# Begin and change of phases of a two-layer graph network laid out anew

## The chip, the cores and the metric

The kernel runs on one core of a Trainium2 chip, in float32. The metric is the device time of one execution in microseconds. Five engines work side by side, each with its own queue of instructions in a fixed order: PE (TensorE: matrix products and transposes), DVE (VectorE), ACT (ScalarE), POOL (GpSimd), and SP (SyncE), which here only issues DMAs.

## The reference

The input `x` is 128 graphs of 64 nodes with 768 features; `adj` is a boolean 64 x 64 matrix for each graph. Both layers are wrapped in a residual and a layer norm.

```python
# layer 0: graph attention with 12 heads of 64, and a gate
h = einsum('bnd,ade->bane', x, W);  th = tanh(h)
a = einsum('bane,aeo->bano', th, w_src) + swap(einsum('bane,aeo->bano', th, w_dst))
a = softmax(where(adj, leaky_relu(a, 0.2), -999.0))
f = elu(einsum('banm,bame->bane', a, h) + b)
g = sigmoid(x @ H_w.T + H_b)
x = layernorm(x + g * f + (1 - g) * x)
# layer 1: self attention with 6 heads of 128
q, k, v = x @ Wq + bq, x @ Wk + bk, x @ Wv + bv
p = softmax(q @ k.T / sqrt(128) + where(adj, 0, -9e15))
x = layernorm(x + (p @ v) @ Wf + bf)
```

## The kernel before

**Tiling.** Two graphs make a tile of 128 tokens (64 tiles), two tiles a pair (32 pairs, numbered 0 to 31). The large products are not computed block by block but in schemes with fewer multiplications: x times [W | H_w] of a pair with 15 products of sums of blocks (class `Stream`, its matrix instructions at L428), x1 times W_v with 7 (class `Product`, L373). For these, sums of blocks are needed: sums over the activations ("S sums", `block_sum` L668 for [W | H_w], `token_sums` L456 for W_v) and sums over the weights (`weight15_sum` L331, 14 for each matrix; `weight_sums` L337, 12 for W_v). The activations' sums run on POOL.

**Two phases.** Phase A does, pair by pair, layer 0 and the product with W_v, whose result goes to DRAM. Phase B does the rest of layer 1, in groups of two pairs. In phase A a pair takes 22 "steps" of PE.

**The order** on every engine is written by hand. `at(step, f)` notes that f is to emit its instructions at a step; all events are sorted by step and run. The steps come from tables: `A_LEAD` and `A_TAIL` for the two tiles of a pair (attention: tanh, dst and src sums, mask, exponentials, scale, aggregate, gate, mix, norm), `A_PAIR` for what a pair shares (loads of x "xb_in", transposes "xT", S sums, loads and transposes of x1), and `MOVED`, offsets for single entries in pairs 0 to 3 and the last three. `BEGIN` holds the steps of the start, `SEAM` those of the change of phases. An engine executes strictly in the resulting order; a waiting instruction holds up all behind it.

**The begin.** Pairs 0 and 1 use plain products, since the weight sums aren't there yet: `plain` (L686) takes h of pair 0 from raw W, `plain_blocks` (L700) h of pair 1 from the blocks, `plain_g` (L715; evicted by DVE at L724) the gate of both. PE transposes H_w's six row blocks (`hw_blocks`, L602), which `load_hrow` (L586) stages in the tile `w2_all`. That tile also holds five blocks of H_w's transpose that the sums would overwrite (`kept_at`), for pair 1's gate, and later the 7 x 1152 columns for W_v and its sums (`weight_plain` L341 loads four blocks: slots 0, 1, 4 and 6). So W_v can load only when all that is no longer needed. Pair 2 is the first whose [W | H_w] product runs in the 15-product scheme, from weight sums made by DVE.

**Around a 15-product step.** Four PSUM tiles ("X") take turns. Each product is evicted by DVE (L746, L748, L757) or by ACT and DVE (L751, then L757), into the tiles xb (h) and hgp (gate). DVE also does the mask (L853), the row maximum (L857), reciprocals (L870), tile transposes of x (L634), the sums over tanh (L799, L808) and the normalization's statistics (L495 to L506). ACT adds (L846) and exponentiates (L862). POOL multiplies with w_dst and w_src (L796, L804), scales the probabilities (L872), and finishes rstd (L507 to L512). PE transposes the probabilities (L883) and aggregates (L901). Attention needs h of the other graph's half in the right partitions, by an exchange DMA (L832, L833), and dst transposed through DRAM (L814, L822).

**The change of phases.** The last pair uses the scheme for W and H_w apart. While its attention and the last two V products run, Wq and Wk load, and their sums (L331, 128 x 256) and those of the first x1 group (L480) are made, all by DVE. ACT then copies at L1437 and the q products (L428, evicted by ACT at L1200 and DVE at L1205) begin.

Of the kernel before, what the change touches and what calls it, by code (L numbers as in the profile page):

```python
# [16 lines left out]
P = 128  # L17
# [33 lines left out]
    -3: 2, 0: 0.5, -1: -1.0, -2: -3,  # L51
}
SEAM = {
    "wq": (15.2, 19.05, 21.41, 19.73, 15.24, 15.81), "wk": (23.61, 26.84, 27.25, 27.56, 31.16, 29.25),
    "wq_sums": (43.53, 43.53, 43.53, 43.53, 44.94, 45.97, 46.03, 46.1, 46.64, 46.71, 48.03, 48.48, 51.7, 53.88),
    "x_sums": (46.57, 48.69, 49.6, 55.88),
    "wk_sums": (51.23, 51.23, 51.93, 52.46, 53.21, 53.21, 54.94, 54.94, 55.54), "x1T": 41.88,
}
BEGIN = {
    "x1_turn": 2.3, "hw": (6.84, 8.48, 10.12, 12.38, 13.26, 14.39),  # L60
    "spread": (1.46, -1.26, -4.37, -2.42, -6.85, -5.31), "h0": (1.02, 3.49, 5.33, 6.0),
    "h1": (8.78, 10.35, 11.68, 13.08, 14.59, 15.89), "g0": (16.99, 17.87, 19.06, 19.8, 19.94, 21.07),
    "g1": (24, 26.46, 26.7, 28, 30.14, 30.91),
    "sums": (16, 16.4, 16.8, 17.2, 17.6, 18, 18.96, 19.36, 19.76, 20.16, 20.63, 21.03, 21.19, 22.66),
    "wv": (31, 30.99, 34.31, 32.04), "v_sums": (34.44, 37, 38, 40.19, 39.85, 40.46, 41.6, 42.47, 44, 45, 46, 47),
}
MOVED = {
    (0, "lead", "add0", None): -1.15, (0, "lead", "dst_in", None): 1.44, (0, "lead", "dst_out", None): 1.44,
    (0, "lead", "dst_sum", None): 1.44, (0, "lead", "exp1", None): 0.42, (0, "lead", "gate", None): 9,
    (0, "lead", "gate_in", None): 1.54, (0, "lead", "mix1", None): -0.33, (0, "lead", "norm1", None): 0.1,  # L70
    (0, "lead", "probs", None): -0.84, (0, "lead", "scale1", None): -0.34, (0, "lead", "src_mul", None): 0.91,
    (0, "lead", "src_sum", None): 1.44, (0, "pair", "S", 0): -2.05, (0, "pair", "S", 1): -2.05,
    (0, "pair", "S", 2): -0.53, (0, "pair", "S", 3): -2.05, (0, "pair", "S", 4): -2.05,
    (0, "pair", "S", 5): -0.11, (0, "pair", "S", 6): -2.05, (0, "pair", "S", 7): -3.68,
    (0, "pair", "S", 8): -2.05, (0, "pair", "S", 9): -2.05, (0, "pair", "S", 10): -2.05,
    (0, "pair", "adj", None): -1.45, (0, "pair", "load", None): 4.57, (0, "pair", "x1T0", None): 2.87,
    (0, "pair", "x1T1", None): 6.05, (0, "pair", "x1_in0", None): 2.1, (0, "pair", "x1_in1", None): 6.5,
    (0, "pair", "x1_sums", 0): 2.1, (0, "pair", "x1_sums", 1): 2.1, (0, "pair", "x1_sums", 2): 2.1,
    (0, "pair", "x1_sums", 3): 1.94, (0, "pair", "xT1", None): 2.9, (0, "pair", "xb_in1", None): 0.77,
    (0, "tail", "aggregate", None): -0.2, (0, "tail", "elu", None): -0.2, (0, "tail", "exchange", None): 0.58,  # L80
    (0, "tail", "gate", None): 8.98, (0, "tail", "norm1", None): 0.17, (0, "tail", "probs", None): -0.41,
    (0, "tail", "scale1", None): -0.2, (0, "tail", "src_sum", None): 2.73, (1, "lead", "add1", None): -0.14,
    (1, "lead", "aggregate", None): 1.47, (1, "lead", "cap", None): -0.86, (1, "lead", "dst_sum", None): 0.36,
    (1, "lead", "elu", None): 1.47, (1, "lead", "exchange", None): 0.15, (1, "lead", "exp0", None): -0.04,
    (1, "lead", "exp1", None): 0.36, (1, "lead", "gate", None): 1.09, (1, "lead", "mask", None): 0.07,
    (1, "lead", "mix1", None): 0.8, (1, "lead", "mix2", None): 0.81, (1, "lead", "probs", None): 1.11,
    (1, "lead", "scale0", None): 0.59, (1, "lead", "scale1", None): 0.59, (1, "lead", "src_mul", None): 0.09,
    (1, "lead", "top", None): 0.07, (1, "pair", "S", 0): -1.23, (1, "pair", "S", 1): 0.55,
    (1, "pair", "S", 2): -0.29, (1, "pair", "S", 3): -2.06, (1, "pair", "S", 4): -0.17,
    (1, "pair", "S", 5): -0.17, (1, "pair", "S", 6): -0.17, (1, "pair", "S", 7): -1.81,  # L90
    (1, "pair", "S", 8): -0.17, (1, "pair", "S", 9): -0.17, (1, "pair", "S", 10): -0.17,
    (1, "pair", "adj", None): -0.68, (1, "pair", "load", None): -1.86, (1, "pair", "x1T0", None): 0.97,
    (1, "pair", "x1_sums", 0): 1.03, (1, "pair", "x1_sums", 1): 1.03, (1, "pair", "x1_sums", 2): 1.03,
    (1, "pair", "x1_sums", 3): 2.18, (1, "pair", "xT0", None): -2.34, (1, "pair", "xT1", None): -0.02,
    (1, "pair", "xb_in0", None): -1.35, (1, "pair", "xb_in1", None): -1.22, (1, "tail", "add0", None): 2.16,
    (1, "tail", "aggregate", None): 0.24, (1, "tail", "cap", None): 2.61, (1, "tail", "dst_in", None): 0.5,
    (1, "tail", "dst_out", None): 0.52, (1, "tail", "dst_sum", None): 0.1, (1, "tail", "elu", None): 0.54,
    (1, "tail", "gate", None): 0.1, (1, "tail", "gate_in", None): 0.1, (1, "tail", "mix1", None): 0.24,
    (1, "tail", "mix2", None): 0.24, (1, "tail", "scale1", None): 1.95, (1, "tail", "spill", None): 0.81,
    (1, "tail", "src_mul", None): 0.1, (2, "lead", "add1", None): -0.55, (2, "lead", "dst_in", None): 0.63,  # L100
    (2, "lead", "dst_out", None): 0.63, (2, "lead", "dst_sum", None): -0.08,
    (2, "lead", "exchange", None): -1.38, (2, "lead", "exp1", None): 1.88, (2, "lead", "gate", None): 2.23,
    (2, "lead", "gate_in", None): 0.63, (2, "lead", "mix1", None): 0.3, (2, "lead", "mix2", None): 0.3,
    (2, "lead", "scale0", None): 0.97, (2, "lead", "spill", None): -0.1, (2, "lead", "src_sum", None): 0.63,
    (2, "lead", "top", None): -0.01, (2, "pair", "S", 0): 0.19, (2, "pair", "S", 1): 0.19,
    (2, "pair", "S", 2): -1.55, (2, "pair", "S", 3): 0.19, (2, "pair", "S", 4): 0.19, (2, "pair", "S", 5): 0.19,
    (2, "pair", "S", 6): 0.19, (2, "pair", "S", 7): 0.19, (2, "pair", "S", 8): 0.19, (2, "pair", "S", 9): 0.37,
    (2, "pair", "S", 10): -0.88, (2, "pair", "adj", None): -6.12, (2, "pair", "load", None): -5.68,
    (2, "pair", "x1T0", None): 0.21, (2, "pair", "x1T1", None): 0.21, (2, "pair", "x1_in0", None): 0.71,
    (2, "pair", "x1_in1", None): 0.47, (2, "pair", "x1_sums", 0): -0.33, (2, "pair", "x1_sums", 1): 0.77,  # L110
    (2, "pair", "x1_sums", 2): 0.33, (2, "pair", "x1_sums", 3): 0.77, (2, "pair", "xT0", None): -0.24,
    (2, "pair", "xb_in0", None): -0.85, (2, "pair", "xb_in1", None): 2.38, (2, "tail", "add0", None): -0.02,
    (2, "tail", "cap", None): 0.97, (2, "tail", "exchange", None): -0.38, (2, "tail", "gate_in", None): -1.09,
    (2, "tail", "mix2", None): 0.18, (2, "tail", "scale0", None): -0.07, (2, "tail", "src_sum", None): 1.37,
    (3, "lead", "add0", None): -2.45, (3, "lead", "gate_in", None): -2.42, (3, "lead", "mix2", None): -0.28,
    (3, "lead", "src_mul", None): 0.39, (3, "pair", "S", 0): -0.05, (3, "pair", "S", 2): -0.21,
    (3, "pair", "load", None): 1.23, (3, "pair", "x1_in0", None): 0.72, (3, "pair", "x1_sums", 0): 1.66,
    (3, "pair", "x1_sums", 1): 1.66, (3, "pair", "x1_sums", 2): 2.33, (3, "pair", "x1_sums", 3): 1.66,
    (3, "pair", "xT0", None): -1.11, (3, "pair", "xb_in0", None): 3.9, (3, "pair", "xb_in1", None): 3.34,
    (3, "tail", "aggregate", None): -0.19, (3, "tail", "cap", None): -2.28, (3, "tail", "dst_in", None): 0.41,  # L120
    (3, "tail", "dst_mul", None): -0.19, (3, "tail", "gate", None): 2.27, (3, "tail", "mix1", None): 0.04,
    (3, "tail", "src_mul", None): -0.33, (3, "tail", "src_sum", None): 1.34, (3, "tail", "tanh", None): -1.24,
    (4, "lead", "dst_mul", None): 0.11, (4, "lead", "exchange", None): -0.73, (4, "lead", "exp0", None): 0.05,
    (4, "lead", "exp1", None): 0.05, (4, "lead", "gate", None): 0.05, (4, "lead", "mask", None): 0.05,
    (4, "lead", "src_sum", None): 0.21, (4, "lead", "top", None): 0.05, (4, "pair", "S", 0): -0.26,
    (4, "pair", "S", 1): -0.26, (4, "pair", "S", 2): -0.26, (4, "pair", "S", 3): -0.26,
# [1424 lines left out]
```

## Time and profile before

| | us |
|---|---|
| time, median of 3 runs | 2821.89 (2819.24 to 2822.54) |
| the profiled execution | 2821.93 |
| its span | 2820.1 |
| PE busy in the span | 2775.9 |
| DVE busy | 1905.0 |
| POOL busy | 1495.9 |
| ACT busy | 1163.1 |

PE is busy for 98% of the span, and the chain that ended last lies on PE for 93%. The mean granted clock of PE was 0.995. A timeline row gives the start and the length of a run of like instructions, the engine, the line, output <- input with shapes, the count, and in brackets the idle time ahead with what ended it. Line numbers in this document are those of the kernel before.

### The profile page before, as it was taken

The numbers are of one execution on the slowest core, as the hardware profiler recorded it, in microseconds if no ns is written. First come the engines' busy times: TensorE is split into PE (matmuls) and PEld (weight loads), VectorE is DVE, ScalarE is ACT, GpSimd is POOL, SyncE is SP. The second block draws the span as 40 slices with busy tenths as digits, with TensorE's granted clock in tenths as the row PEclk, the third lists the DMA queues.
The fourth block names the chain that finished last, engine by engine and source line by source line (L and its number), as shares of the span: only waits on it lengthen the run. The fifth ranks groups of instructions, "written<-read, shape, count | busy, mean of one in ns | idle before, by whom it ended". The sixth has DMA issues, their size and how long they took to land.

```text
span 2820.1 us, 50020 instructions
## 1 busy us (share of the span) xinstructions
PE 2775.9 (98%) x17544; PEld 1958.7 (69%) x17544; DVE 1905.0 (68%) x4026; ACT 1163.1 (41%) x3685; POOL 1495.9 (53%) x1791
## 2 busy tenths in 40 slices
PE   8899999999999999999799999999999999999998
PEld 7445545555555555555578888888888888888887
DVE  4888888888888888888754555555555555555556
ACT  4466565665666665665622221122221222211223
POOL 1656556555555565565455645445645445554455
PEclk9999999999999999999899999999999999999999
DMA  5454454454454454444631221221221222211222
GB/s 147 126 151 136 136 152 130 133 154 131 133 157 134 133 150 132 140 150 132 174 130 35 91 81 65 70 91 58 91 73 63 80 65 84 91 68 58 91 85 74
DMA packets 358682, 308.36 MB, mean 109 GB/s; under 512 B 226592, under 2 KB 304160, under 8 KB 358432
## 3 DMA queue, kind: packets, MB, share of 16 engines
q1 hardware_dynamic: 358144, 304.77, 35.2%
q8 instruction: 140, 2.29, 0.3%
q14 instruction: 110, 0.90, 0.1%
q10 hardware_dynamic: 288, 0.39, 0.0%
HBM read 191.41 MB, written 101.06 MB: 104 GB/s over the span
## 4 chain that ended last, share of the span: by engine, by line
PE 93%; DVE 3%; DMA 1%; POOL 1%; ACT 1%; SPq 0%; issue 0%; POOLq 0%; DVEq 0%; ACTq 0%
PE X L428 70%; PE X L373 15%; PE pa L901 2%; PE pb L1326 2%; PE pb L1244 2%; PE pa L883 1%; PE pb L1302 1%; PE X L715 1%; PE X L700 1%; POOL Sc L1190 0%; DMA w<-in_L_gnn_Wv_dram 0%; DVE s L853 0%; ACT s L862 0%; DMA hb_bc<-in_L_gnn_H_b_dram 0%; DVE T L634 0%
## 5 line engine op out<-in xcount | busy, mean ns | idle before, releaser
L428 PE MATMUL X<-S,w 128*128 128x256 f32 x2752 | 636.5, 380 | 0.0
L428 PE MATMUL X<-w,S 128*128 128x512 f32 (+1 forms) x1364 | 598.9, 584 | 10.7 <-POOL S L668 7.5
L428 PEld LDWEIGHTS X<-S,w 128*128 128x128 f32 x2752 | 519.1, 190 | 68.5
L428 PEld LDWEIGHTS X<-w,S 128*128 128x128 f32 x1364 | 254.9, 191 | 289.8 <-issue 241.0
L1222 DVE TENSOR_TENSOR xs<-xs,X 128x256 f32<-128x256 f32 x512 | 209.6, 418 | 175.1 <-PE X L428 166.9
L872 POOL TENSOR_TENSOR s<-s,rs 128x384 f32<-128x384 f32 x128 | 106.9, 836 | 372.1 <-DVE rs L870 355.9
L428 PE MATMUL X<-w,Sc 128*128 128x256 f32 x1280 | 294.4, 381 | 0.1
L1205 DVE TENSOR_TENSOR k<-k,X 128x256 f32<-128x256 f32 x320 | 132.6, 417 | 232.4 <-PE X L428 160.6
L373 PE MATMUL X<-w,S 128*128 128x384 f32 x768 | 270.9, 490 | 1.5 <-POOL S L456 1.4
L428 PEld LDWEIGHTS X<-w,Sc 128*128 128x128 f32 x1280 | 241.5, 190 | 34.1 <-DVE xs L1222 0.9
L1205 DVE TENSOR_TENSOR q<-q,X 128x256 f32<-128x256 f32 x320 | 132.9, 419 | 195.0 <-PE X L428 155.0
L428 PE MATMUL X<-xb,w 128*128 128x256 f32 x1024 | 258.6, 383 | 0.8 <-ACT q L1200 0.8
L862 ACT ACTIVATE s<-s,nmx 128x64 f32<-128x64 f32 x768 | 254.8, 335 | 6.8 <-DVE nmx L857 6.8
L516 ACT ACTIVATE xs<-xs,shift,rstd 128x768 f32<-128x768 f32 x62 | 63.5, 1025 | 435.8 <-POOL shift L512 416.0
L428 PE MATMUL X<-w,T 128*128 128x512 f32 (+1 forms) x496 | 223.9, 583 | 5.7 <-DVE xb L757 3.4
L1200 ACT ACTIVATE k<-X,bk_c 128x256 f32<-128x256 f32 x192 | 90.9, 473 | 316.4 <-PE X L428 316.4
L846 ACT ACTIVATE s<-s,src 128x64 f32<-128x64 f32 x768 | 196.6, 338 | 37.6 <-DMA s<-dst_d 34.2
L428 PEld LDWEIGHTS X<-xb,w 128*128 128x128 f32 x1024 | 192.2, 190 | 28.4 <-ACT q L1200 1.2
L757 DVE TENSOR_TENSOR hgp<-hgp,X 128x512 f32<-128x512 f32 (+1 forms) x235 | 150.6, 651 | 80.8 <-PE X L428 67.2
L1200 ACT ACTIVATE q<-X,bq_c 128x256 f32<-128x256 f32 x192 | 90.8, 473 | 276.7 <-PE X L428 276.7
L373 PEld LDWEIGHTS X<-w,S 128*128 128x128 f32 x768 | 141.1, 190 | 90.1 <-POOL S L456 1.6
L1190 POOL TENSOR_TENSOR w<-cT 128x256 f32<-128x256 f32 x32 | 23.3, 727 | 334.2 <-PE X L428 332.9
(143 smaller groups left out, 4893.1 us busy)
## 6 DMA issues: line engine op xcount, KB each, us to landing
xb<-in_x_dram SPq DMA_DIRECT2D x64, 384.0 KB
s<-dst_d SPq DMA_DIRECT2D x128, 192.0 KB
x_d<-xb SPq DMA_DIRECT2D x64, 384.0 KB
xT_d<-T SPq DMA_DIRECT2D x64, 384.0 KB
v_d<-v SPq DMA_DIRECT2D x128, 192.0 KB
xb<-xT_d SPq DMA_DIRECT2D x32, 768.0 KB
xb<-v_d SPq DMA_DIRECT2D x256, 96.0 KB
xs<-x_d SPq DMA_DIRECT2D x64, 384.0 KB
```

Source lines behind the costliest of these rows:

```text
L373: nc.tensor.matmul(o, self.lhsT(i, c), rhs, start=first and c == 0, stop=last and c == CH - 1, skip_group_check=True,)
L428: nc.tensor.matmul(ps, self.lhsT(r, slot, c), self.rhs(r, slot, c), start=start and c == 0, stop=stop and c == 1, skip_group_check=True,)
L516: nc.scalar.activation(r, r, AF.Identity, bias=shift, scale=rstd)
L757: nc.vector.tensor_tensor(o, o, view(ps), ALU.add if positive else ALU.subtract)
L846: nc.scalar.activation(self.s[:, a], self.s[:, a], AF.Prelu, bias=self.src[:, a : a + 1], alpha=LEAKY_ALPHA,)
L862: nc.scalar.activation(self.s[:, a], self.s[:, a], AF.Exp, bias=self.nmx[:, a : a + 1], accum_out=self.sm[:, a : a + 1],)
L872: nc.gpsimd.tensor_tensor(t, t, rs[:, :, None].to_broadcast([P, A // 2, S]), ALU.mult)
L901: nc.tensor.matmul(self.pos[h2][own, j, :], self.pt[rws, j, own], rhs, start=True, stop=True,)
L1200: nc.scalar.activation(o[:, b], ps, AF.Identity, bias=bias[:, hd : hd + 1], scale=1.0 if positive else -1.0)
L1205: nc.vector.tensor_tensor(o[:, b], o[:, b], ps, ALU.add if positive else ALU.subtract)
L1222: nc.vector.tensor_tensor(o, o, ps, ALU.add if positive else ALU.subtract)
L1244: nc.tensor.matmul(pc[own, q, i, j, :], qT[:, b, q, own], kT[:, b, q, own], start=True, stop=True,)
```

## The change

Four things change together.

1. `load_hrow` puts the rows 0 to 4 of H_w at offsets inside the slots that W_v's blocks take, and row 5 in a tile of its own; `kept_at` moves into slots that only W_v's sums take. W_v's loads then have to wait only for the transposes of rows 0 to 4, and their steps go from 31-34 to 16-19.
2. The four buffers "snap" become one tile "snaps" of the same size, whose quarters `snap` takes in turn. Pair 2's transposes of x go into it instead of into T tiles, and its loads of x, transposes and S sums come some ten steps sooner. A list of the loaded x tiles becomes an entry by tile; pair 1's second tile is loaded first.
3. Each weight sum has an engine: in the begin, 2 of the 14 sums of [W | H_w] go to POOL, and of W_v's 12, which were all on POOL, 4 go to DVE. In the change of phases 6 of the 14 sums for Wq, 5 of the 9 early ones for Wk and 1 of the 4 sums of x1 go from DVE to POOL.
4. The steps of BEGIN, SEAM and MOVED are new. On PE, the first transposes of H_w rows come ahead of the last h products of pair 0; the first two aggregations (L883, L901) move by some groups of the gate's products. For the last pairs, the mask L853 of a tile stands before two evictions instead of after, L799 and L801 before the statistics, rstd behind two L456, and the last exchange comes sooner. In the pairs between, the order is practically the old one.

```diff
-    -3: 2, 0: 0.5, -1: -1.0, -2: -3,
+    -3: 2, 0: 0.5, -1: 0.5, -2: -3,
...
 SEAM
-    "x_sums": (46.57, 48.69, 49.6, 55.88),
+    "x_sums": (47.3, 49.42, 52.14, 57.17),
...
+    "q_on": (0, 0, 1, 1, 1, 0, 0, 0, 1, 0, 1, 1, 0, 0), "x_on": (0, 1, 0, 0),
+    "k_on": (1, 1, 0, 1, 1, 0, 1, 0, 0),
...
 BEGIN
-    "x1_turn": 2.3, "hw": (6.84, 8.48, 10.12, 12.38, 13.26, 14.39),
+    "x1_turn": 1.91, "hw": (2.1, 5.84, 9.65, 13.05, 14.38, 15.55),
...
-    "wv": (31, 30.99, 34.31, 32.04), "v_sums": (34.44, 37, 38, 40.19, 39.85, 40.46, 41.6, 42.47, 44, 45, 46, 47),
+    "wv": (16.38, 18.07, 18.64, 16.34), "on": (0, 0, 0, 1, 0, 0, 0, 0, 1, 0, 0, 0, 0, 0),
+    "v_on": (1, 0, 1, 1, 0, 1, 1, 1, 0, 1, 1, 0),
+    "v_sums": (33, 33.8, 34.6, 35.4, 36.2, 37, 37.8, 38.6, 39.4, 40.2, 41, 41.8),
...
 MOVED
-    (2, "pair", "S", 2): -1.55, (2, "pair", "S", 3): 0.19, (2, "pair", "S", 4): 0.19, (2, "pair", "S", 5): 0.19,
+    (2, "pair", "S", 2): -11.5, (2, "pair", "S", 3): -9.76, (2, "pair", "S", 4): -9.76, (2, "pair", "S", 5): -9.76,
...
-    (2, "pair", "xT0", None): -0.24
+    (2, "pair", "xT0", None): -9.24, (2, "pair", "xT1", None): -9, (2, "pair", "xb_in0", None): -8.3,
...
         def load_hrow(oc):
-            hrows[oc] = w2_all[:, oc * D : (oc + 1) * D]
+            o = (0, D, 2 * D, 6 * D, 9 * D)
+            hrows[oc] = k3.tile([P, D], F32, name="pt") if oc == 5 else w2_all[:, o[oc] : o[oc] + D]
...
         def kept_at(slot):
-            t = w2_all[:, NC * D :]
             k = KEPT.index(slot)
-            return t[:, k * 512 : (k + 1) * 512].rearrange("p (c o) -> p c o", c=2)
+            o = 3 * D + k * 512 + (k == 4) * (7 * D + 384 - 3 * D - 4 * 512)
+            return w2_all[:, o : o + 512].rearrange("p (c o) -> p c o", c=2)
...
-        def turn(xp):
-
-            dst = k3.tile([P, NC, P], F32, name="T", bufs=4)
+        def turn(xp, dst=None):
+
+            if dst is None:
+                dst = k3.tile([P, NC, P], F32, name="T", bufs=4)
...
+        snaps = k1.tile([P, 4 * HALF], F32, name="snaps")
+        n_snap = [0]
+
         def snap(k, ps):
-            t = k1.tile([P, HALF], F32, name="snap", bufs=4)
+            n = n_snap[0] % 4
+            n_snap[0] += 1
+            t = snaps[:, n * HALF : (n + 1) * HALF]
...
-            at(BEGIN["sums"][n], lambda k=k: weight15_sum(whg, k, nc.vector, slice(0, 512)))
+            eng = (nc.vector, nc.gpsimd)[BEGIN["on"][n]]
+            at(BEGIN["sums"][n], lambda k=k, eng=eng: weight15_sum(whg, k, eng, slice(0, 512)))
...
-                    lambda c=c, k=k: weight_sums(lambda s: w2[:, s, c], nc.gpsimd, [k]),
+                    lambda c=c, k=k: weight_sums(
+                        lambda s: w2[:, s, c], (nc.vector, nc.gpsimd)[BEGIN["v_on"][4 * c + k]], [k]
+                    ),
...
             def xb_in(d, i):
-                d.setdefault("xp", []).append(blocks(x_t[2 * d["p"] + i]))
+                d["xb", i] = blocks(x_t[2 * d["p"] + i])
...
             def xT(d, i):
-                d.setdefault("T", []).append(turn(d["xp"][i]))
+                dst = snaps[:, i * D : (i + 1) * D].rearrange("p (c n) -> p c n", n=P) if d["p"] == 2 else None
+                d.setdefault("T", []).append(turn(d["xb", i], dst))
...
+        ENG = (nc.vector, nc.gpsimd)
...
-            at(o + SEAM["wq_sums"][k], lambda k=k: weight15_sum(early[0], k, nc.vector, slice(0, P)))
+            at(o + SEAM["wq_sums"][k], lambda k=k: weight15_sum(early[0], k, ENG[SEAM["q_on"][k]], slice(0, P)))
...
-            at(o + SEAM["x_sums"][k], lambda k=k: group_sum(early_sums, k, nc.vector, EARLY[k]))
+            at(o + SEAM["x_sums"][k], lambda k=k: group_sum(early_sums, k, ENG[SEAM["x_on"][k]], EARLY[k]))
...
-            at(o + SEAM["wk_sums"][k], lambda k=k: weight15_sum(early[1], k, nc.vector, slice(0, P)))
+            at(o + SEAM["wk_sums"][k], lambda k=k: weight15_sum(early[1], k, ENG[SEAM["k_on"][k]], slice(0, P)))
```

## The prediction

> **What bounds the kernel now.** I read the windows of busy time first, then the waits of PE, then the timeline of each engine around every wait of PE over 0.3 us. The profiled execution took 2821.93 us: a span of 2820.1 and 1.83 outside it. It stands 0.04 above the median of 2821.89, so a sum made against it holds for the median. PE is busy 2775.9 us of the span, which leaves 44.2 idle. The windows (columns: stretch, length, busy us of PE, PEld, DVE, ACT, POOL with instructions, clock, DMA share, GB/s) say where:
>
> ```profile
> 80.00:120.00 40.00, 30.67 (x123) 14.45 (x121) 28.65 (x40) 17.70 (x66) 28.91 (x34) 0.96 0.64 189
> ...
> 1360.00:1400.00 40.00, 30.41 (x247) 20.32 (x246) 31.79 (x59) 27.66 (x106) 18.25 (x19) 0.92 0.66 192
> 1400.00:1440.00 40.00, 35.78 (x162) 21.58 (x160) 28.97 (x57) 10.15 (x28) 11.27 (x11) 0.91 0.56 187
> ```
>
> Every window of 40 us from 160 to 1320 and from 1480 to 2760 shows PE busy for all 40. About 18 us of idle lie in the first 160 us, 19 between 1320 and 1480 (the change of phases), 7 at the end. The change touches the first two places and, from the order of instructions, almost nothing between. So at most some 37 us of idle, and the slow clock after it, can be won. PE's timeline in the begin (start, length, line, and in brackets the wait ahead and what ended it):
>
> ```profile
> 82.56 3.60 PE L428 MATMUL X<-w,S 128*128 128x512 f32 x8
> 86.00 1.88 PE L428 MATMUL X<-w,T 128*128 128x512 f32 x4
> 89.40 1.96 PE L428 MATMUL X<-w,S 128*128 128x512 f32 x4 [1.53 <-ACT xb L751]
> 95.98 5.40 PE L428 MATMUL X<-w,S 128*128 128x512 f32 x8 [4.62 <-POOL S L668]
> ...
> 120.19 3.42 PE L428 MATMUL X<-w,T 128*128 128x512 f32 x4 [3.37 <-DVE xb L757]
> ```
>
> After a wait PE also runs slow: eight items take 5.40 at 95.98 and 3.60 at 82.56; four take 3.42 at 120.19 and 1.88 at 86.00. So the wait of 4.62 costs 6.4, that of 3.37 costs 4.9 and a little behind it (4.34 for the next twelve items against 4.03): 5.2.
>
> The first wait's cause is on POOL, the second's is on DVE, in these rows of their timelines:
>
> ```profile
> 93.53 0.99 POOL L337 TENSOR_TENSOR w<-w 128x384 f32<-128x384 f32 x1 [2.08 <-DMA w<-in_L_gnn_Wv_dram]
> 94.49 2.12 POOL L668 TENSOR_TENSOR S<-T 128x256 f32<-128x256 f32 x2
> ```
>
> ```profile
> 111.83 5.85 DVE L853 TENSOR_TENSOR s<-s,cap 128x768 f32<-128x768 f32 x1
> ```
>
> A sum of W_v waits for its load, issued only at 82.19 because its place held rows still read by the gate of pair 1, and stands ahead of pair 2's S sums. Then L853 takes 5.85 where its median over 64 is 0.947: POOL runs L337 and L456 without a gap from 109.17 to 116.88. The products' evictions L748 and L757 stand behind L853.
>
> PE in the change of phases:
>
> ```profile
> 1354.59 1.13 PE L428 MATMUL X<-w,T 128*128 128x256 f32 x4 [1.91 <-DVE hgp L757]
> ...
> 1380.43 6.07 PE L373 MATMUL X<-w,S 128*128 128x384 f32 x18 [1.42 <-POOL S L456]
> ...
> 1402.71 0.90 PE L883 MATMUL pa<-ident,s 128*128 128x128 f32 x3 [2.25 <-POOL s L872]
> ...
> 1439.20 1.13 PE L428 MATMUL X<-xs,w 128*128 128x256 f32 x4 [1.70 <-ACT xs L1437]
> ```
>
> Between 1389 and 1403 PE waits five times for the softmax chains of the last two tiles. There the limit is a chain of latencies over ACT, DVE and POOL, not one engine's work.
>
> **The change, part by part: the begin.** The matrix instructions are the same 7620 in another order, so only waits count.
>
> *H_w rows moved, W_v loads earlier.* The four loads (2.96 us of issue on SP, row 82.19) move to about 46-52, behind the transposes of H_w rows 0 to 4 and in SP's order behind tile 1's dst and s. The exchange of tile 0 (issues from 48.70, landed some 2 us on) stands behind three of them and comes at about 49 to 53; PE asks for it at about 61. Pair 2's eight loads of x (0.65 each) go ahead of tile 1's dst, where SP was idle from 34.6 to 43. W_v took 8.84 us to land; the DMA has room then (share 0.23 in 40 to 80). Nothing waits.
>
> *Pair 2's transposes and S sums ten steps earlier.* They write into the snap tile, idle until the first V product. The 11 sums (0.72 each) run on POOL between 57 and 76, where it was idle from 58.22+1.77 to 73.98. The 4.62 wait goes: **-6.4**.
>
> *First h product of pair 1.* Tile 1's x is now loaded ahead of tile 0's. The last of these loads landed at 28.12, and tile 0 is transposed first (two of 0.65), then tile 1 (two more): the first product can start at about 29.9 instead of 29.00, and of the blocks put before it 0.5 cover: **+0.4** (0 to +1.0).
>
> *First L883 three groups earlier, two weight sums on POOL.* The row nearest to a 128x1024 sum on POOL is L796, 1.81 for 768 elements, so about 2.4. The first L872 stands behind the first of them, its reciprocal behind four sums of DVE; PE comes there at about 55.7, and L872 ended at 55.5 before. Taken **+0.8**, from 0 to +1.9 (the second half behind one more DVE sum of 1.21 and L872's 0.83).
>
> *First eviction of pair 2.* DVE is gapless here, so what stands ahead of L748 counts. PE's last group before HG now follows the aggregation of tile 3 directly: L923 twice, L724, L808 (0.94), L935, L936, L944, L945 (0.98 each), statistics and rstd (1.4), one W_v sum now on DVE (0.55), L748 (0.4). From the end of the gate's last group that is 7.5; the eviction on ACT follows at 7.9, PE has three steps (5.2) and waits about 2.7 instead of 1.53: **+1.2** (0 to +4). The wait is now as long as those which PE followed slowly (2.66 was followed by 3.56 for eight items of 1.89, 1.91 by none): **+1.5** (0 to +1.8).
>
> *The second wait.* Eight W_v sums on POOL (0.99) instead of 12, begun at about 95, four on DVE (0.55), so that POOL is through with them by 101. The L456 four still run at 107-111, when L853 of tile 4 comes. Here a rule must be weighed.
>
> The row: L853 5.85 while five or six POOL sums passed. The Trainium skill, SBUF — State Buffer, section "SBUF: two separate sides", says that a DVE operation with two SBUF inputs and a reading GpSimd operation exclude each other for one whole instruction, whoever started first. Other rows fit: L872 took 1.77 at 58.22 beside one DVE sum of 1.22, and 0.83 at 54.66 beside a reduction. By the rule L853 can lose one L456 (1.0) and PE, with about that much slack, waits for nothing: -5.2. By the row it can lose four in series, L853 ends at 112.3, evictions by 114 and PE stands for 3: -1. I take a wait of 1.0 without a slow restart, near the rule since POOL's queue has a third fewer sums: **-4.2** (-5.2 to 0).
>
> Sum of the begin: -6.4 + 0.4 + 0.8 + 1.2 + 1.5 - 4.2 = **-6.7**.
>
> **The change of phases.** The mask L853 of a tile of pair 30 stands before two L757 instead of after them (0.4 each), so exponentials leave ACT sooner for the eviction behind the 1.91 wait: **-0.8** (-0.8 to 0). The rstd of that pair on POOL, which waited 0.90 and took 1.1, moves behind two L456: the 1.42 wait goes, **-1.4** (0 to -1.4); its ACT reader is 2 us later, which nothing on the last chain needs. L799 goes ahead of the statistics (1.4 us of DVE), but its input ends at 1374.6 on POOL: about 1 us earlier dst, mask and scale of the last but one tile. The exchange issued sooner removes the 1.14 us wait at 1395.84, but the next L883 waits for the last chain anyhow, so only the chain's shift counts: **-1.0** (+0.5 to -2).
>
> *Twelve sums from DVE to POOL at the end.* 11 of L331 (0.37 on DVE in the row 1434.95 4.01 x11, 0.75 on POOL by 0.73 for L668's 256 elements) and one L480 (0.68; on POOL by 1.81 for 768, 512 take 1.27). DVE gets 11 x 0.37 + 0.68 = 4.7 us back in a stretch where it ended at 1439.5 and PE waited 1.70. POOL was idle from 1425.3 to 1447.8, so its 11 x 0.75 + 1.27 = 9.5 fit. They also stand ahead of two L456 for the last V (1.5 later each; PE reads the fourth only after 1429). The wait of 1.70 goes, the 0.80 behind it (q's eviction) I leave: **-1.7** (-2.5 to +4.8).
>
> A rule speaks against it: the Trainium skill, Perfetto Trace Analysis, section "Optimizing Scalar/DVE Operations", warns that the two share an SBUF read port and moving work between them may not help. The rows agree that they exclude each other: two DVE operations (0.96 alone) and two POOL sums (1.00 alone) took turns from 1404.01 to 1408.03, 4.02 us for 3.92 of work.
>
> ```profile
> 1404.01 1.50 DVE L944 SCALAR_TENSOR_TENSOR hgp<-hgp 128x768 f32<-128x768 f32 x1
> 1405.54 1.63 DVE L945 SCALAR_TENSOR_TENSOR xb<-xb,hgp 128x768 f32<-128x768 f32 x1
> ```
>
> By the rule the DVE would lose 9.5 for 4.7 and the wait would grow by 4.8. But DVE has holes there (4.73 before 1426.19, 2.69 before 1430.69) that take POOL's share, and the five wk sums are due only later; hence the gain. Sum: -0.8 - 1.4 - 1.0 - 1.7 = **-4.9**.
>
> Together -6.7 - 4.9 = -11.6: 2821.93 - 11.6 = **2810.3**.
>
> **The rivals.** (1) *The change of phases gives nothing and the new wait before the first eviction costs more*: DVE's sums, blocked by the POOL sums and S sums moved among them (4.8 + 7 more x 0.72 = 9.8 us of POOL, less the 2.4 that DVE is spared), run up to 7.4 late, of which about 4.2 are covered because the aggregation comes later too; up to 3.2 more at L748. For it: DVE has no gap from 46.8 to 80. Against: half of its work there has a PSUM input or one input. -6.7 + 3.2 + 0 = -3.5: 2818.
>
> (2) *All waits fall*: the second wait gone wholly (-1.0), no slow restart (-1.5), L883 unhindered (-0.8), and the seam's chain 2 shorter with its slow clock (windows at 0.91 and 0.92) a third better, about -4. That is -19: 2803. Against: chain and clock need every link to move.
>
> (3) *Slower: the shared port decides at both ends.* L748 3.2 later, L853 held by four sums again (the 4.2 not won), and at the end of the seam POOL's 9.5 us block DVE by 4.8 with a slow restart of 1.5 and the 3.2 of the seam's other gains lost in the same way. -6.7 + 3.2 + 4.2 + 1.5 (more restart) = +2.2 and +6.3: +8.5, so 2830. For it: 5.85 once in the trace. Against: the holes named. It decides from the point where L853 again takes over 4 us and DVE's last weight sum ends after 1441.
>
> **How the numbers follow.** A measurement of this kernel can tell 0.2% (5.6 us) from no change. Forecast 0.52 (own range 2805 to 2816), rival 1 0.23, rival 2 0.14, rival 3 0.11. Faster by more than 0.2% (below 2816.3): the forecast, rival 2 and a small part of rival 1, 0.68. Within: most of rival 1, 0.22. Slower: rival 3, 0.10. The range reaches from 2801 to 2823: it takes in rivals 1 and 2 and leaves out rival 3 and a tail below.
>
> **What would show it.** Right: no wait for S L668 near 96; L853 of tile 4 under 2 us; a wait of 2 to 4 us near 91 for ACT's first eviction of pair 2; no wait for xs before the first q product; PE busy in the window 80 to 120 at 35 or more. Wrong: first L872 on POOL later than 56; L853 over 4; DVE's last weight sum before q later than in before; an idle PE in the windows between 160 and 1320.

## The result

The changed kernel takes 2814.18 us (median of 18 runs, 2811.16 to 2816.87), the kernel before 2820.11 (18 runs beside it, 2815.91 to 2822.54). The ratio is 0.9981, 95% interval 0.9974 to 0.9988: 5.9 us less by the medians, about the 0.2% (5.6 us) that the prediction took for the least that can be told. The forecast was 2810.3, a gain of 11.6 us, with a range of 2801 to 2823. The direction was right and the time lies in the range, but half of the gain isn't there.

The two profiled executions lie further apart than the medians: 2812.34 us (span 2810.5) after, 2821.93 before. The windows of the changed kernel, in the columns used above:

```profile
80.00:120.00 40.00, 36.00 (x140) 17.77 (x139) 36.17 (x62) 24.00 (x89) 25.55 (x27) 0.96 0.44 130
...
1360.00:1400.00 40.00, 28.52 (x183) 16.94 (x182) 30.98 (x54) 24.79 (x94) 19.96 (x22) 0.83 0.87 246
1400.00:1440.00 40.00, 37.49 (x183) 25.26 (x183) 27.61 (x51) 10.74 (x22) 16.78 (x20) 1.00 0.56 194
```

PE gained 5.3 us of busy time between 80 and 120, and lost 1.9 between 1360 and 1400. The times of the second row are shifted by the 8 us already won, so places are compared below by landmarks, not by windows. PE's timeline in the begin, of the changed kernel (its line L464 is L428 of before, L794 is L751, L409 is L373):

```profile
91.58 7.11 PE L464 MATMUL X<-w,S 128*128 128x512 f32 x12 [4.00 <-ACT xb L794]
...
115.69 4.03 PE L409 MATMUL X<-w,T 128*128 128x384 f32 x12
```

Both waits that the prediction set out to remove are gone, 4.62 and 3.37. One new wait of 4.00 stands in the place of 1.53, and twelve items after it take 7.11 us, where twelve such items took 5.31 at 151.42 in before. The first V product begins at 115.69 instead of 123.41.

The change of phases in the changed kernel (L926 is L883, L915 is L872, L672 is L634, L1485 is L1437):

```profile
1384.53 0.55 PE L926 MATMUL pa<-ident,s 128*128 128x128 f32 x3 [1.76 <-POOL s L915]
...
1389.77 0.90 PE L926 MATMUL pa<-ident,s 128*128 128x128 f32 x3 [3.55 <-POOL s L915]
1392.59 0.90 PE L926 MATMUL pa<-ident,s 128*128 128x128 f32 x3 [1.91 <-POOL s L915]
1395.88 4.21 PE L409 MATMUL X<-w,T 128*128 128x384 f32 x6 [2.39 <-DVE T L672]
...
1431.11 1.13 PE L464 MATMUL X<-xs,w 128*128 128x256 f32 x4 [1.71 <-ACT xs L1485]
```

The wait of 1.91 is gone and that of 1.42 is 0.22. But the waits on the softmax chain grew, a new one of 2.39 stands before a V product, and the wait for xs is what it was, 1.71.

Four landmarks measure the places separately in each of the fourteen profiles (the experiments below name the kernels; "seam" is the change of phases): the start of pair 0's first V product ("V0"), of the last pair's first product ("W31"), of the first q product ("Q"), and the end. All in us:

| profile of | V0 at | V0 to W31 | W31 to Q | Q to end |
|---|---|---|---|---|
| before | 123.41 | 1212.20 | 100.00 | 1384.49 |
| before, second profile | 122.82 | 1213.66 | 100.33 | 1384.49 |
| old begin, new seam | 118.94 | 1212.67 | 100.78 | 1383.41 |
| after | 115.69 | 1212.04 | 99.78 | 1382.99 |
| new begin, old seam | 115.86 | 1211.46 | 99.23 | 1382.65 |
| after, seam's sums on DVE | 117.34 | 1212.47 | 102.16 | 1383.13 |
| after, begin's sums on old engines | 117.94 | 1211.69 | 102.26 | 1383.21 |
| after, last V spill early | 116.08 | 1211.66 | 102.25 | 1381.91 |
| after, first eviction ahead | 118.00 | 1211.69 | 98.16 | 1382.75 |
| before, pair 2 early | 121.07 | 1212.59 | 100.04 | 1383.20 |
| before, W_v early | 121.33 | 1212.24 | 100.26 | 1382.77 |
| new begin, old seam, first eviction ahead | 117.66 | 1211.46 | 99.12 | 1384.46 |
| after, Wq's loads at old steps | 117.30 | 1211.67 | 103.90 | 1382.93 |
| after, all three | 115.80 | 1211.72 | 102.21 | 1382.87 |

Two profiles of the same kernel can differ by 1.5 us in one column, so a single profile shows which waits there are, and the medians show what they are worth.

### The profile page after: what moved, and what is told of

The parts are those of the page before. It is cut to its first block, busy times and chain, and to the rows that moved or that the text cites. A ratio compares the mean times of both kernels' runs of the same rounds, so it can differ in the third digit from the quotient of the medians.

```text
span 2810.5 us, 50021 instructions
## 1 busy us (share of the span) xinstructions
PE 2771.6 (99%) x17544; PEld 1957.4 (70%) x17544; DVE 1901.8 (68%) x4016; ACT 1163.8 (41%) x3685; POOL 1515.2 (54%) x1801
## 4 chain that ended last, share of the span: by engine, by line
PE 94%; DVE 2%; POOL 1%; SPq 1%; DMA 1%; issue 1%; ACT 0%; POOLq 0%; DVEq 0%; ACTq 0%
PE X L464 70%; PE X L409 15%; PE pa L944 2%; PE pb L1374 2%; PE pb L1292 2%; PE pa L926 1%; PE pb L1350 1%; PE X L743 1%; PE X L758 1%; POOL Sc L1238 0%; SPq L664 0%; DMA x_d<-xb 0%; POOL w L839 0%; DMA wd_bc<-in_L_gnn_w_dst_dram 0%; POOL S L711 0%
## 5 line engine op out<-in xcount | busy, mean ns | idle before, releaser
L464 PE MATMUL X<-S,w 128*128 128x256 f32 x2752 | 635.3, 379 | 0.0
L464 PE MATMUL X<-w,S 128*128 128x512 f32 (+1 forms) x1364 | 599.1, 584 | 9.0 <-ACT xb L794 4.0
L464 PEld LDWEIGHTS X<-S,w 128*128 128x128 f32 x2752 | 518.1, 190 | 68.0
L464 PEld LDWEIGHTS X<-w,S 128*128 128x128 f32 x1364 | 256.1, 191 | 287.5 <-issue 242.6
L915 POOL TENSOR_TENSOR s<-s,rs 128x384 f32<-128x384 f32 x128 | 107.1, 838 | 358.4 <-DVE rs L913 343.1
L464 PE MATMUL X<-w,Sc 128*128 128x256 f32 x1280 | 294.4, 381 | 0.1
L409 PE MATMUL X<-w,S 128*128 128x384 f32 x768 | 271.1, 490 | 0.4 <-POOL S L492 0.2
L464 PEld LDWEIGHTS X<-w,Sc 128*128 128x128 f32 x1280 | 241.5, 190 | 34.1 <-DVE xs L1270 0.9
L464 PE MATMUL X<-xb,w 128*128 128x256 f32 x1024 | 258.0, 382 | 0.8 <-ACT q L1248 0.8
L464 PE MATMUL X<-w,T 128*128 128x512 f32 (+1 forms) x480 | 215.2, 581 | 0.5 <-DVE hgp L800 0.4
L464 PEld LDWEIGHTS X<-xb,w 128*128 128x128 f32 x1024 | 192.0, 190 | 28.3 <-ACT q L1248 1.2
L409 PEld LDWEIGHTS X<-w,S 128*128 128x128 f32 x768 | 140.9, 190 | 88.5 <-POOL S L492 0.8
```

Source lines behind the costliest of these rows:

```text
L409: nc.tensor.matmul(o, self.lhsT(i, c), rhs, start=first and c == 0, stop=last and c == CH - 1, skip_group_check=True,)
L464: nc.tensor.matmul(ps, self.lhsT(r, slot, c), self.rhs(r, slot, c), start=start and c == 0, stop=stop and c == 1, skip_group_check=True,)
L915: nc.gpsimd.tensor_tensor(t, t, rs[:, :, None].to_broadcast([P, A // 2, S]), ALU.mult)
```

## The experiments

### Is the kernel before the same in every execution?

> The kernel before, unchanged, profiled a second time. Its 18 times fall into two groups, six at 2815.9 to 2817.5 and twelve at 2819.2 to 2822.5. Theory B (which of DVE's mask L853 and POOL's sums comes first differs from one execution to the next): the group is that of L853 at 111 us; either the time lies at about 2820.5 with L853 near 5.8 us and a PE wait of about 3.4 us near 120, or at about 2816.3 with L853 under 2 us and no such wait. Theory A (the hold is there in every execution, the two groups come from elsewhere): L853 near 5.8 us whatever the time is.

It took 2823.10 us, a little above the upper of the two groups, and the hold is there. L853 and the wait behind it, from the timelines of DVE and PE in this second profile of before:

```profile
110.03 6.70 DVE L853 TENSOR_TENSOR s<-s,cap 128x768 f32<-128x768 f32 x1
```

```profile
119.24 3.78 PE L428 MATMUL X<-w,T 128*128 128x512 f32 x4 [4.17 <-DVE xb L757]
```

The profile of the old begin with the new change of phases (next section) has the same orders of instructions here, and its L1111, the same mask, took 1.23, with no wait of PE at that place:

```profile
112.39 1.23 DVE L1111 TENSOR_TENSOR s<-s,cap 128x768 f32<-128x768 f32 x1
```

That execution took 2817.60, near the lower group, and reached V0 4 us sooner. So the hold comes in some executions of one and the same begin (two of three profiles) and not in others. The one profile that the prediction worked from had it. That the two groups of times are those with and without it fits all three profiles, but it is not shown: three are few, and the groups are not clean. Of some 130 later executions of before, 18 lie between 2817.5 and 2819.2, where the first 18 left a gap.

### The two halves of the change

```diff
 begin_only: the changed kernel with
+MOVED: pairs 0 to 3 new, the last three pairs old;  SEAM, V_MOVED old
 seam_only: the kernel before with
+MOVED: pairs 0 to 3 old, the last three pairs new;  SEAM, V_MOVED, engines of the seam's sums new
```

> The changed kernel's begin (new places for H_w rows and W_v, pair 2's early transposes, the engines of the sums of the begin, the steps of pairs 0 to 3) with the old steps and engines of the last three pairs and of the change of phases. Theory A (the recorded sum): -6.7 us against the kernel before, so about 2813.5. Theory B: the begin is worth about -7.7 against an execution in which L853 was held, -3.5 against one in which it was not, about -6 against the median of the kernel before, which is all that the whole change brings.

> The old begin with the changed kernel's steps and engines of the last three pairs and of the change of phases. Theory A (the recorded sum): -4.9 us. Theory B (the softmax chain ends some 2 us sooner, but PE then waits for the transposed x1 of pair 30, and the wait for xs before the first q product is the same): between -2 and +0.5 us. The profile also looks a third time at L853 of the old begin, as in the first run.

The begin alone: 2812.80 us, ratio to before 0.9978 (0.9970 to 0.9987), about -6.2 us. The change of phases alone: 2819.07, ratio 0.9997 (0.9989 to 1.0005), not told from zero. The begin brings all that the change brings. The part for which -4.9 was forecast gives nothing that can be measured, which is what theory B expected.

### What in the begin does it: each half alone

```diff
 pair2_early: the kernel before with snaps, turn(xp, dst) and
+    (2, "pair", "S", n): -8.3 to -11.5, (2, "pair", "xT0"): -9.24, "xT1": -9, "xb_in0": -8.3, "xb_in1": -9.51
 wv_early: the kernel before with load_hrow and kept_at at the new places and
+    "wv": (16.38, 18.07, 18.64, 16.34)
```

> The kernel before with one part of the change alone: pair 2's x loaded and transposed sooner into the snap tile and its S sums ten steps sooner; W_v still loads at about 82 us, sums on their old engines. Theory A (recorded): the wait of 4.6 us for S goes with its slow restart, about -6.4 us, whatever W_v does. Theory B: the same wait goes, but DVE and POOL take turns and the first eviction comes later, so -3 to -5 us; the late W_v sums on POOL still meet L853.

> The kernel before with the other part alone: H_w rows and kept blocks at their new places and W_v's loads sooner; pair 2's S sums stay late. Theory A: the W_v sum on POOL no longer waits 2.1 us for its load, so the PE wait of 4.6 us shrinks by 2 to about 2.5 us, the slow restart stays: about -2 us. Rival: S sums still stand behind the W_v sum and rstd, PE clock is lost anyhow, 0 us.

Neither gives anything: 2818.48 us, ratio 1.0002 (0.9994 to 1.0011), and 2818.33, ratio 0.9997 (0.9988 to 1.0005). Both parts did what they were to do, and the time came back elsewhere.

With pair 2's sums early, the wait for S is gone. But POOL's S sums now meet DVE's 14 weight sums, DVE falls behind, its reciprocals come 3 us later, and PE, which in the old order asks for the probabilities one group of the gate's products sooner than in the new (75.00 against 77.55), waits for them. From PE's timeline of that kernel (L1115 is L883):

```profile
78.03 0.81 PE L1115 MATMUL pa<-ident,s 128*128 128x128 f32 x3 [2.55 <-POOL s L1104]
80.18 0.90 PE L1115 MATMUL pa<-ident,s 128*128 128x128 f32 x3 [1.35 <-POOL s L1104]
```

The first 15-product step begins at 89.00 instead of 82.56: the two waits are 3.9 of the 6.4 us, and the granted clock was 0.83 between 70 and 90.

With W_v early, the wait for S shrinks as expected (1.78 instead of 4.62), but W_v's sums on POOL still stand beside L853 (here L858). DVE's timeline, and PE's behind it:

```profile
107.42 7.83 DVE L858 TENSOR_TENSOR s<-s,cap 128x768 f32<-128x768 f32 x1
```

```profile
117.75 3.78 PE L432 MATMUL X<-w,T 128*128 128x512 f32 x4 [4.15 <-DVE xb L762]
```

The hold, the longest of all, takes the second wait from 3.37 to 4.15. So the gain of the begin is not the sum of its parts. Read from these two profiles, it needs three things together: room on POOL for the S sums, the reordered aggregations on PE, and W_v's sums out of L853's way. No run took these three apart.

### The engines of the begin's sums

```diff
-    "on": (0, 0, 0, 1, 0, 0, 0, 0, 1, 0, 0, 0, 0, 0), "v_on": (1, 0, 1, 1, 0, 1, 1, 1, 0, 1, 1, 0),
+    "on": (0,) * 14, "v_on": (1,) * 12,
```

> The changed kernel with its weight sums of the begin on their old engines: all 14 of [W | H_w] on DVE, all 12 of W_v on POOL, in the new order. Theory A (recorded): two more sums on DVE (2.4 us) reach the first eviction only in part, POOL's four more sums meet L853 again: +1 to +4 us against the changed kernel. Rival (the port makes DVE and POOL take turns, so it does not matter who runs a sum): within 1 us.

2815.36 us, ratio to before 0.9989 (0.9981 to 0.9998), against 0.9981 (0.9974 to 0.9988) for the whole change. That is 1.2 us more by the medians and 2.3 by the ratios, but the intervals overlap. Theory A lies at its lower edge and the rival a little outside its own bound: not settled. L853's counterpart took 1.73 here; twelve sums on POOL alone did not bring the long hold back in this profile.

### The sums of the change of phases, and what xs waits for

```diff
 seam_dve: the changed kernel with
-    "q_on": (0, 0, 1, 1, 1, 0, 0, 0, 1, 0, 1, 1, 0, 0), "x_on": (0, 1, 0, 0), "k_on": (1, 1, 0, 1, 1, 0, 1, 0, 0),
+    "q_on": (0,) * 14, "x_on": (0,) * 4, "k_on": (0,) * 9,
 last_spill_early: the changed kernel with, in the V product's sink,
-                nc.sync.dma_start(v_d[2 * d["p"] + i][:, halves(half)], o)
+                if d["p"] < NP - 1 or k < 3:
+                    nc.sync.dma_start(v_d[2 * d["p"] + i][:, halves(half)], o)
+                if d["p"] == NP - 1 and k == 0:
+                    i, half = PLACE[3]
+                    nc.sync.dma_start(v_d[2 * d["p"] + i][:, halves(half)], o)
```

> The changed kernel with all sums of the change of phases on DVE again (12 sums, in the same steps). Theory A (DVE's sums hold up the copies to xs): +1.7 us against the changed kernel. Theory B (the copies wait for something else, most likely the spill of the last V block that lies where xs goes): within 0.5 us of the changed kernel, the PE wait before the q product stays at 1.7 us and the copies start about 2.9 us after the first q product in both.

> The changed kernel in which the last block of V is written to DRAM from another block's tile, some 14 us sooner (so that block of V is wrong in the output), and the last tile is not read by any DMA. Theory B (xs waits for the last V spill): the copies to xs start at once after the V product before, about 1.2 to 1.7 us sooner, and the PE wait of 1.7 us before the q product falls to under 0.5: -1 to -2 us. Theory A (they wait for the weight sums): no change.

With all twelve sums back on DVE the time is 2813.94 us, ratio 0.9981 (0.9974 to 0.9987): the same as the changed kernel. The copies to xs begin 2.9 us after the first q product in before (1438.53 behind 1435.61), after (1430.44 behind 1427.51) and here (1434.90 behind 1431.97), whoever made the sums. In all three the profile puts the wait down to the weight sum L331, on DVE or POOL:

```profile
1430.44 2.18 ACT L1485 COPY xs<-xb 128x512 f32<-128x512 f32 x4 [2.25 <-POOL w L367]
```

That row is of the changed kernel. The second kernel leaves the last V block unwritten: its DMA takes another block's tile, which was ready sooner, and that part of the output is wrong. There the same copies begin 0.99 after the first q product (1430.98 behind 1429.99), and the row names another releaser:

```profile
1430.98 2.18 ACT L1489 COPY xs<-xb 128x512 f32<-128x512 f32 x4 [0.31 <-DMA v_d<-v]
```

So what held them was the spill (the write to DRAM) of the last V block, presumably because its tile lies where xs is written. The weight sum was merely the last semaphore that the profile could name. Of the 1.94 us, 1.08 is left in the profile: from Q to the end it takes 1381.91, the shortest of all, against 1382.99 in after. PE now waits 1.46 for an x1 sum of DVE (its line L516 is L480 of before) that the old wait had covered. The time is 2812.67, ratio 0.9977 (0.9971 to 0.9984), 1.5 us less by the medians, with overlapping intervals: a gain is not shown.

### The new wait in the begin

```diff
-    (0, "tail", "norm1", None): 0.17,      "v_sums": (33, 33.8, 34.6, ...
+    (0, "tail", "norm1", None): 0.78,      "v_sums": (33, 34.3, 34.6, ...
```

> The changed kernel with the statistics and rstd of tile 1 and one W_v sum of DVE moved behind the first eviction of pair 2 (on POOL, rstd behind the w_dst product); nothing else. If what DVE does ahead of that eviction sets the new wait: 2.0 us less stands ahead (1.4 of statistics, 0.55 of the sum), the wait of 4.0 near 91 falls to about 2.0, and its slow restart (1.8) may go: -2 to -3.8 us against the changed kernel. Rival (the eviction waits for its product or for ACT): no change.

The same on the new begin with the old change of phases:

> The new begin with the old change of phases, and the first eviction put ahead as in evict_first. If both effects are as said, it beats both kernels: 2812.8 of the begin alone less 2 to 3.8, 2809 to 2811.

The wait fell from 4.00 to 3.46 and 3.47, not to 2.0, and in the first of the two kernels a second one came four items later:

```profile
95.61 5.40 PE L464 MATMUL X<-w,S 128*128 128x512 f32 x8 [1.93 <-ACT xb L794]
```

DVE's and POOL's timelines of that kernel show where 1.5 of the 2.0 us went:

```profile
87.46 2.44 DVE L987 SCALAR_TENSOR_TENSOR xb<-hgp,xb 128x768 f32<-128x768 f32 x1
```

```profile
86.74 2.35 POOL L839 TENSOR_TENSOR w<-th,wd_bc 128x768 f32<-128x768 f32 x1 [1.12 <-ACT th L835]
```

With rstd behind it, POOL's w_dst product L839 runs at 86.74 instead of 91.68. There it meets the four mixing operations of DVE (0.96 each when alone), and L987 takes 2.44. The second wait comes over ACT, whose order was not changed: its normalization, which needs rstd, stands ahead of the second eviction (L794), so with rstd later it runs at 94.26 instead of 91.76, and the eviction at 95.19 instead of 92.69. In the second kernel that wait is only 0.34, but the four items behind the first take 3.57. Measured: 2812.43 us (5 runs, ratio 0.9968, 0.9956 to 0.9981) on the changed kernel, 2813.48 (8 runs, 0.9973, 0.9963 to 0.9984) on the begin alone, which without it had 2812.80. By the ratios both are a little lower than without (0.9968 against 0.9981, 0.9973 against 0.9978), but the intervals overlap and V0 is no sooner (118.00 and 117.66): no gain is shown.

### The loads of Wq and Wk

```diff
 wq_old:
-    "wq": (15.2, 20.88, 20.96, 19.74, 19.3, 19.87),
+    "wq": (15.2, 19.05, 21.41, 19.73, 15.24, 15.81),
 all_three: evict_first, wq_old and
-    "wk": (23.61, 27.31, 27.72, 28.03, 33.3, 30.87),
+    "wk": (23.61, 31.0, 31.2, 31.4, 33.3, 30.9),
```

> The changed kernel with Wq's six loads at their old steps: only SP's order changes, three of them now issue about 5 us sooner, one instead of three directly ahead of the reload of x1 of pair 30. Theory C (the moved loads compete with that reload; DVE's transposes wait for it, and the second reciprocal of the softmax behind them): the reload lands 1 to 3 us sooner, the PE wait for the second half of the last but one tile's probabilities falls from the 4 to 5.5 us seen in four of five profiles with the new change of phases to 2 or less, -1.5 to -3 us. Rival (the reload's time is that of writing x1 and reading it back): no change.

> The changed kernel with the first eviction put ahead, Wq's loads at their old steps, and the loads of Wk that stood right behind the second reload of x1 moved behind the write of its transpose. Theory C: both reloads of pair 30 land sooner, the PE wait of 2 us for the transposed x1 falls to under 1: 2808 to 2811. Rival: equal to evict_first.

Theory C falls in this form: 2815.68 us, ratio 0.9985 (0.9979 to 0.9992), and 2816.01, ratio 0.9986 (0.9979 to 0.9992); the direction is that of a loss, though neither can be told from the changed kernel. The PE wait went to 6.67 and 5.95 us, not to 2, the one for the transposed x1 stayed at 2.75 and 2.49, and from W31 to Q it took 103.90 and 102.21, the first the longest of all. SP's timelines, first of the changed kernel, then with Wq's old steps:

```profile
1371.23 1.09 SPq L865 DMA_DIRECT2D s<-dst_d  x2
1372.86 0.34 SPq L1005 DMA_DIRECT2D x_d<-xb  x1
1373.25 1.61 SPq L356 DMA_DIRECT2D w<-in_L_gnn_Wq_dram  x3
```

```profile
1374.92 1.09 SPq L865 DMA_DIRECT2D s<-dst_d  x2
1376.06 0.58 SPq L356 DMA_DIRECT2D w<-in_L_gnn_Wq_dram  x1
1376.70 0.47 SPq L1005 DMA_DIRECT2D x_d<-xb  x1
```

With three loads of Wq ahead of dst's way through DRAM (issued at 1368.61, against 1368.05), its read-back could issue 3.7 us later. The write of x1, its reload and the exchange stand behind it on SP. The loads collide with a chain of DMAs either way; by these profiles the changed kernel's place is the better one.

## Why the prediction was half right

**The two waits of the begin** ("the 4.62 wait goes: -6.4", "-4.2" for the second): both went, the second wholly, where the sum had left a wait of 1.0; in the profile that is -6.4 and -5.2. The mask of tile 4 took 1.22. But the base was mis-sized: the profile of before was one with the hold. From that one profile to that of after, V0 is 7.7 us sooner. From the mean of three profiles of the old begin (121.7) to the mean of five of the new begin with its own orders (115.69 to 117.34, mean 116.5) it is 5.3; forecast -6.7. The times say -6.2. That the begin's sum came so near is in part luck: the second wait gave 1.0 more than written and the two terms below 1.2 more, the first eviction took 1.6 more, and some executions of before had less to give.

**The first h product and the first L883** ("+0.4", "+0.8"): the first cost nothing, g0 starting at 47.35 instead of 47.39. L883 found its input ready. The reciprocal stood at 51.43 on DVE, 3 us sooner than before, because it moved ahead of DVE's weight sums, behind four of them instead of six. The prediction had put the first POOL sum into that wait; it was through by 42.5 (2.36 us, estimated 2.4).

**The first eviction** ("+1.2", "+1.5"): right in kind, too small. The wait is 4.00, +2.5, and the slow restart +1.8. The list of work on DVE ahead of the eviction was right (its entries sum to 8.6 us, it took 8.8, from 82.31 to 91.10), but not when it begins: the 7.5 behind PE's last group has L923 (L966 below) done within that group. POOL's timeline of the changed kernel:

```profile
75.90 1.44 POOL L711 TENSOR_TENSOR S<-snaps 128x256 f32<-128x256 f32 x1
77.30 2.52 POOL L839 TENSOR_TENSOR w<-th,wd_bc 128x768 f32<-128x768 f32 x1
```

and DVE's:

```profile
79.86 0.95 DVE L842 TENSOR_REDUCE sd<-w 128x12 f32<-128x768 f32 x1 [1.37 <-POOL w L839]
...
82.31 1.01 DVE L966 TENSOR_TENSOR xb<-pa,b_bc 128x384 f32<-128x384 f32 x2
```

The early S sums push L839 back, DVE's mixing operations and it take turns (2.52 for 1.81), DVE stands 1.37 for the result, and L966, ready with the aggregation at 79.5, starts at 82.31. This is rival 1's mechanism, with less than half of its price of 3.2: the wait is 1.3 longer than the forecast 2.7.

**The change of phases** ("-4.9"): this failed, and is the other half of the miss. Of its four steps, two waits did go as said: 1.91 is absent or 0.3, and 1.42 is 0.2 in the profiles with the new orders. What they gave was spent again in two places.

The first is the mask that now stands ahead of two evictions. It runs beside an S sum that PE waits for. That sum takes 1.32 instead of 0.72, PE waits 0.96 for it, and 24 items behind go slowly, 6.46 instead of 5.34. DVE's, POOL's and PE's timelines of the changed kernel:

```profile
1334.44 1.03 DVE L896 TENSOR_TENSOR s<-s,cap 128x768 f32<-128x768 f32 x1
```

```profile
1334.74 1.32 POOL L711 TENSOR_TENSOR S<-S,T 128x256 f32<-128x256 f32 x1
```

```profile
1336.11 2.07 PE L464 MATMUL X<-w,S 128*128 128x256 f32 x4 [0.96 <-POOL S L711]
...
1339.69 6.46 PE L464 MATMUL X<-w,S 128*128 128x256 f32 x24
```

So PE is past the place of the 1.91 wait 20.0 us behind W31, as in before. In the eight profiles with the new orders it is 18.3 to 20.1, in the six with the old ones 19.3 to 20.0: the "-0.8" is there in some and gone in others.

The second is the softmax chain, where the prediction had written -1.0. The step that failed is "only the chain's shift counts". (Of the five waits that it read there, four were for the chain; the fifth, 1.14, was for the exchange.) DVE's timeline, of the changed kernel with the seam's sums on DVE, whose orders around this place are those of the changed kernel:

```profile
1382.64 0.18 DVE L916 RECIPROCAL rs<-sm 128x6 f32<-128x6 f32 x1
1386.98 1.25 DVE L675 STREAM_TRANSPOSE T<-xp 128x384 f32<-128x384 f32 x2 [4.16 <-DMA xp<-x_d]
1388.15 0.15 DVE L916 RECIPROCAL rs<-sm 128x6 f32<-128x6 f32 x1
```

The second reciprocal of tile 62 (the last but one) stands behind the transposes of x1, and these wait for the reload of x1 through DRAM. In before the same transposes waited 0.71 us; now they are reached sooner, but the reload isn't: 1.45 in the profile of after, 4.16 here, 5.78 with Wq's old steps. PE's wait for that half of the probabilities goes with it: 1.76, 5.05 and 6.67. Over the profiles it was 0.24 to 1.18 with the old change of phases (six profiles), and 1.76 to 5.50 with the new (six, without the two with Wq's old steps).

In the profile of after this wait is the shortest, and the chain does end sooner: its last probabilities come 64.9 us behind W31, 67.1 in before. But the V product behind them needs the second pair of transposes, and they wait for the second reload, 1.04 in before and here:

```profile
1395.14 1.26 DVE L672 STREAM_TRANSPOSE T<-xp 128x384 f32<-128x384 f32 x2 [3.52 <-DMA xp<-x_d]
```

PE waits 2.39 and begins that product 68.2 us behind W31, 68.0 in before. From W31 to Q the old orders took 99.1 to 100.3, the new ones 98.2 to 102.3, and 102.2 and 103.9 with Wq's old steps. So what the earlier links won was spent on the slow stretch, or on waiting for a transfer that the forecast had not put on the chain. No run took the transposes from ahead of the reciprocal; that this alone would give the gain back was not tried.

**The sums moved to POOL at the end** ("-1.7"): wrong at the root. The wait for xs was read from its row as a wait for DVE's sums; it is the last V spill, and the engine of the sums makes no difference.

**The rules weighed.** The warning that work moved between DVE and POOL may bring nothing fits the change of phases (ratio 0.9981 with and without), though there the sums were not what was waited for. For L853 the trace goes beyond the page's "whole instruction": see below.

**The rivals.** Rival 1 (the seam gives nothing, the first eviction comes later, 2818) named both mechanisms of what happened and was too dear by 4 us. Its "no gap from 46.8 to 80" on DVE overlooks a hole of 0.91 ahead of 60.54. Rival 3's end of the seam, DVE held up by POOL's sums, did not occur.

## What to carry to other kernels

A wait's named releaser is the last semaphore, not always the cause: before a saving is written against it, look for a DMA that reads the place being overwritten, and compare the offset of the waiting instruction in several profiles. When links of a chain are pulled ahead, list on each engine what stands between them and waits for a transfer; the gain ends at the first such wait. Before summing against one profiled execution, profile the same kernel again: a wait that is there in one execution and not in the next is worth only its share. And when an operation of DVE is moved, look at what it will run beside on POOL, and who waits for that.

## What the hardware showed

A DVE operation with two SBUF inputs can be held by a queue of POOL sums for far longer than one of them lasts. L853 (0.95 alone) took 5.85, 6.70 and 7.83 us in three profiles, each time until POOL's row of 1.00 us sums without a gap came to its end. In two more profiles with the same row of sums (old begin with new seam, pair 2 early) it took 1.23 and 1.22: a POOL sum of 1.7 stood directly behind, so there they took turns. The Trainium skill, SBUF — State Buffer, section "SBUF: two separate sides", lets the one that started first have the port for its instruction; these rows show the waiting one passed over five or more times.

One difference shows in the traces: how late in the running POOL sum DVE came. Before's L853 came at 111.83, with 0.27 us of this sum left:

```profile
111.10 1.00 POOL L456 TENSOR_TENSOR S<-T 128x384 f32<-128x384 f32 x1
```

In the other two that were held it was 0.16 and 0.33. In the old begin with the new seam it came at 112.39, with 0.41 of the first of these sums left:

```profile
111.80 1.00 POOL L595 TENSOR_TENSOR w<-w 128x384 f32<-128x384 f32 x1
112.77 1.71 POOL L714 TENSOR_TENSOR S<-S,T 128x384 f32<-128x384 f32 x1
```

In all fourteen profiles, 38 DVE operations of this size came with 0.40 or more left of a 1.00 us sum that another followed at once, and each waited for that one sum only. That fits the nine profiles with the new begin: none of them is held, and there L853's counterpart always came with 0.40 or more left. If this is what decides, a shift of a quarter of a microsecond between two executions is enough. It is an observation and no rule: no run moved the moment alone, and beside shorter POOL sums (0.73) DVE came with 0.25 left and was not held.
